# Layer 0's feed-forward and half of its return gathers are placed between the steps of layer 1's attention

## The chip, the core and the metric

The kernel runs on one core of a Trainium2 chip. The core has five engines that run side by side, each through its own instructions in order: TensorE (PE in the profile; its weight loads are PEld), VectorE (DVE), ScalarE (ACT), GpSimd (POOL) and SyncE (SP, which here only issues DMAs). Matrix products land in PSUM, which has 8 banks of 128 x 512 floats; everything else is in SBUF. The metric is the device time of one execution in microseconds (us), and the median of nine runs is taken.

## What is computed

A stack of four "gated" layers runs over x, 16 batches of 128 tokens with 128 features, with a context of the same shape. Each layer adds tanh(gate) times a cross-attention block and then tanh(gate) times a feed-forward block, both of a layer norm of x. The part that matters here is:

```
x = x + tanh(g_xattn[0]) * L0_xattn(layernorm(x), ctx)   # top 2 of 8 experts for each token
x = x + tanh(g_ffn[0])   * L0_ffn(layernorm(x))          # relu, hidden values rounded to fp8, output to fp16
x = x + tanh(g_xattn[1]) * L1_xattn(layernorm(x), ctx)   # 16 heads of 8, softmax in blocks of 64 keys
x = x + tanh(g_ffn[1])   * L1_ffn(layernorm(x))          # 8 components, the largest logit chooses
```

Layer 0's first block routes each token, by its context row, to two of eight experts. Its feed-forward has 512 hidden values. Layer 1's attention has 16 heads over 128 keys, with a maximum and a sum for each block of 64 keys. Layer 2 needs a table of position vectors, which are gathered row by row long before it and turned (transposed) on the way.

## The kernel before, in words

The 16 batches are taken in 4 chunks of 4 (NJ = 4, BJ = 4). The program is written in Tile: the order of the instructions on each engine is chosen by a scheduler from the order in the text and from its own estimates, except where a wrapper (class `InOrder`, L28) tells it to keep the order of the text. Before, only layer 1's feed-forward and one later layer are wrapped.

**Layer 0's experts** (`l0_xattn`, L293). The tokens are sorted by expert into 39 blocks of 128 rows. A one-hot tile `of` (L388) is built to find each block's tokens; 32 matmuls read it. Then for each block the rows are gathered by GpSimd (L454), the expert's first weights are fetched by SyncE into a ring of 7 (`w1`, L438, 258 KB each), and the result rows are written to a buffer in HBM (L499).

**The way back** (`l0_returned`, L506). For a batch b, GpSimd gathers from that buffer the rows of each token's first and second expert (two gathers, L512), and VectorE adds each, weighted, to x[b] (L519). A gather is told to start only behind the addition two before it (`k.behind`, L516), and there are 4 buffers.

**Layer 0's feed-forward** (`l0_ffn`, L544), chunk by chunk. `hidden(j)` norms the chunk (`layernorm`: statistics, a square root on ScalarE, xn on VectorE, four transposes, a copy), multiplies it by the first weights (4 matmuls of 128 x 512) and rounds to fp8 on ScalarE. `output(j)` has 16 fp8 matmuls, an addition of the bias (`l0f_y`) and an addition to x. Chunk 0's return gathers stand ahead of the loop; the gathers of the following chunk stand between the matmuls of each chunk, and 6 of the 17 turns of positions (`turn_positions`) too. PSUM is split here into 4 + 2 + 2 banks.

**Layer 1's attention** (`l1_xattn`, L593), one pass over 16 batches in eight stages, each some steps behind the one before, with all 8 banks in one rotation. In the prediction the stages go by the names of their tiles:

- `queries` (L670): every fourth step, `project` norms the next chunk and computes its queries and keys (matmuls by Wq and Wk), `project_values` the values; in every step, GpSimd spreads queries and keys over the heads (`l_qz`, `l_kz`, L663).
- `maxima` (L681): scores by 4 matmuls, then four reductions on VectorE into `l_top` (L690). Each step releases one gather of position rows (`pe<-in_L_xattn_rpe`, L961; `k.gather`).
- `turned`: `l_top` is transposed, copied by ScalarE, and GpSimd makes `l_mz` of it (L703).
- `weights` (L708): scores minus maxima by 8 matmuls, exponentials on ScalarE (`l_a`, L722).
- `values`, `normed` (divides by the sums, `l_y`, L748, and releases another gather of position rows), `output`, `projected` (matmul by Wo, addition to x).

Layer 1's feed-forward (`l1_ffn`) follows. There GpSimd subtracts and adds in pairs, VectorE takes a running maximum of which each releases a gather of position rows as long as any of the 65 is left, and the rest of the turns lie between.

Of the kernel before, what the change touches and what calls it, by code (L numbers as in the profile page):

```python
# [18 lines left out]
P = 128  # L19
NB = 16  # L20
# [7 lines left out]
class InOrder:  # L28


    def __init__(self, tc, engine):
        self.tc, self.engine, self.last = tc, engine, None
# [18 lines left out]
class Engines:  # L51


    def __init__(self, tc, nc):
        self.nc = nc
        self.tensor, self.vector, self.scalar, self.gpsimd = (
            InOrder(tc, e) for e in (nc.tensor, nc.vector, nc.scalar, nc.gpsimd)
        )

    def __getattr__(self, name):  # L60
        return getattr(self.nc, name)
# [2 lines left out]
class Kernel:  # L64
# [27 lines left out]
        return self.psum.tile([P, 512], F32, tag=tag, name=f"ps_{tag}", bufs=self.bufs[tag])  # L92

    def w2k(self, name):
        return self.work.tile([P, 512], F32, tag="w2k", name=name, bufs=13)

    def sq(self, name, dtype=F32):
        return self.small.tile([P, P], dtype, tag="sq", name=name, bufs=14)
# [182 lines left out]
def pipeline(n, *stages):  # L281


    kept = {}
    for t in range(n + max(lag for _, lag in stages)):
        for s, (fn, lag) in enumerate(stages):
            u = t - lag
            if 0 <= u < n:
                kept[u, s] = fn(u, kept.pop((u, s - 1))) if s else fn(u)
# [3 lines left out]
def l0_xattn(k):  # L293
# [91 lines left out]

    blockb = k.sm([P, 2 * NB], "l0_blockb", BF16, bufs=1)
    nc.vector.tensor_copy(blockb, block)
    of = k.work.tile([P, 2 * NB, 2, NBLK], BF16, tag="l0_of", name="l0_of", bufs=1)  # L388
    nc.vector.tensor_tensor(
        of[:, :, 1], bc(along[:, 0:NBLK].unsqueeze(1), [P, 2 * NB, NBLK]), bc(blockb.unsqueeze(2), [P, 2 * NB, NBLK]),  # L390
        ALU.is_equal,
# [114 lines left out]
def l0_returned(k, b):  # L506


    nc = k.nc
    for i in range(2):  # L510
        y = k.small.tile([P, P], F32, tag="l0_xs", name="l0_back", bufs=4)
        dma = nc.gpsimd.indirect_dma_start(  # L512
            out=y, out_offset=None, in_=k.l0_out_d,
            in_offset=bass.IndirectOffsetOnAxis(ap=k.l0_rows[:, 2 * b + i : 2 * b + i + 1].bitcast(U32), axis=0),
        )
        if len(k.l0_added) > 1:  # L516
            k.behind(dma, k.l0_added[-2])
        k.l0_added.append(
            nc.vector.scalar_tensor_tensor(  # L519
                k.x[:, b, :], y, k.l0_w[:, b, i : i + 1], k.x[:, b, :], ALU.mult, ALU.add  # L520
            )
        )
# [21 lines left out]
def l0_ffn(k):  # L544

    nc = k.nc
    w1 = k.load("L0_ffn_w1T", [P, 512], tag="ffn_w1")
    b1 = k.load("L0_ffn_b1T", [P, NF])  # L550
    w2 = k.load("L0_ffn_w2T", [P, NF, P], "(c p) d -> p c d", tag="ffn_w2", p=P)
    b2 = k.load_rows("L0_ffn_b2", P, tag="ffn_b2")
    wq, bq = k.wts.tile([P, NF, P], FP8, name="l0_wq"), k.wts.tile([P, P], F16, name="l0_bq")
    nc.vector.tensor_copy(wq, w2, saturate=False)
    nc.vector.tensor_copy(bq, b2)
    k.l0_added = []
    l2_gates_of_ctx(k)
    for b in range(BJ):
        l0_returned(k, b)

    def hidden(j):
        k.layernorm(j)
        hq = k.work.tile([P, NF, N], FP8, tag="w4k", name="l0f_q", bufs=3)
        for f in range(NF):
            ph = k.ps("mm")
            k.mm(ph, w1[:, f * P : (f + 1) * P], k.chunk(k.xnT, j))
            nc.scalar.activation(hq[:, f, :], ph, AF.Relu, bias=b1[:, f : f + 1], saturate=False)
            if j + 1 < NJ:
                l0_returned(k, BJ * (j + 1) + f)
            if j and f % 2:  # L570
                turn_positions(k, 2 * (j - 1) + f // 2)
        return hq

    def output(j, hq):
        py = k.ps("acc")
        for i in range(BJ):
            for f in range(NF):
                k.mm(
                    py[:, i * P : (i + 1) * P], hq[:, f, i * P : (i + 1) * P], wq[:, f, :],
                    start=f == 0, stop=f == NF - 1,  # L580
                )
        y = k.work.tile([P, N], F16, tag="w2k", name="l0f_y", bufs=13)
        nc.vector.tensor_tensor(
            y.rearrange("p (b d) -> p b d", b=BJ), py.rearrange("p (b d) -> p b d", b=BJ),
            bc(bq.unsqueeze(1), [P, BJ, P]), ALU.add,
        )
        k.add_chunk(j, y, 4)

    pipeline(NJ, (hidden, 0), (output, 1))

def l1_xattn(k):  # L593

# [3 lines left out]


    nc = k.nc
    k.banks(bank=8)
    H, DH, G = 16, 8, 4
    scale = DH**-0.5
    wq, wk, wv, wo = (k.load(f"L1_xattn_W{n}T", [P, P], tag=f"W{n}") for n in "qkvo")
    by_h = lambda t: t.rearrange("p (h s) -> p h s", h=4)
    neg = k.const.tile([P, 4], F32, name="l1_neg")

    nc.gpsimd.memset(neg, -1.0)  # L610
    for g in range(G):
        rows = neg[32 * g : 32 * g + 32, :]
        nc.gpsimd.affine_select(
            out=rows, in_=rows, pattern=[[-2, 4]], compare_op=ALU.is_ge, fill=0.0, base=0, channel_multiplier=1
        )
        nc.gpsimd.affine_select(
            out=rows, in_=rows, pattern=[[2, 4]], compare_op=ALU.is_ge, fill=0.0, base=1, channel_multiplier=-1
        )

# [13 lines left out]
    two = k.wts.tile([P, 2, BJ, H, 32], F32, tag="w16b", name="l1_v")  # L633
    vs = [two[:, n] for n in range(2)]
    for v in vs:
        nc.gpsimd.memset(v, 0.0)
        nc.gpsimd.memset(v[0:64, :, :, DH : DH + 1], 1.0)
        nc.gpsimd.memset(v[64:P, :, :, 2 * DH + 1 : 2 * DH + 2], 1.0)
    qkT = {}

    def project(j):
        k.layernorm(j)
        qkT[j] = (k.w2k("l1_qT"), k.w2k("l1_kT"))
        for out, w, src in zip(qkT[j], (wq, wk), (k.xnT, k.ctxT)):
            pq = k.ps("mm")
            k.mm(pq, w, k.chunk(src, j))
            nc.scalar.copy(out, pq)
# [20 lines left out]
        return out  # L668

    def queries(b):  # L670
        if b == 0:
            project(0)
            project_values(0)
        if b % BJ == 2 and b // BJ + 1 < NJ:
            project(b // BJ + 1)
        if b % BJ == 3 and b // BJ + 1 < NJ:

            project_values(b // BJ + 1)
        return masked(b)

    def maxima(b, qk):  # L681
        qz, kz = qk
        j, i = divmod(b, BJ)
        top = tops[b % 3]
        ss = [k.ps("mm") for _ in range(G)]
        for g in range(G):
            rows = slice(32 * g, 32 * g + 32)
            k.mm(ss[g], qkT[j][0][rows, i * P : (i + 1) * P], kz[rows, :])
        for g in range(G):
            done = nc.vector.tensor_reduce(  # L690
                top[:, 32 * g : 32 * g + 8], ss[g].rearrange("p (n s) -> p n s", n=8), AX.X, ALU.max
            )
        k.gather(done)
        return qz, top

    def turned(b, qt):
# [82 lines left out]
    for t in range(NB + 6):  # L779
        for fn, lag in stages:  # L780
            b = t - lag
            if 0 <= b < NB:
                args = (state.pop((after[fn], b)),) if fn in after else ()
                state[fn, b] = fn(b, *args)
        if t == NB + 1:

            xn = k.work.tile([P, BJ, P], F32, tag="w4k", name="l1f_xn", bufs=3)
            k.layernorm(0, keep=xn, pow=k.half)

def l1_ffn(k):
# [105 lines left out]
    for s in range(C * NJ + 24):  # L898
# [19 lines left out]
        for m, i in ms:  # L918
# [9 lines left out]
            elif i == C + 3:  # L928
                for fn, half in (
# [1 line left out]
                    (added, 1),  # L931
                ):
                    fn(m, half)
        if s % 2 and s // 2 <= P // 8 - 6:
            turn_positions(k, s // 2 + 6)
        for n in pieces.get(s, []):
            if n not in under_way:
                under_way[n] = k.norm(n[1], pow=k.half)
# [774 lines left out]
        k.add_chunk(j, y, 7)  # L1713


LAYERS = [l0_xattn, l0_ffn, l1_xattn, l1_ffn, l2_xattn, l2_ffn, l3_xattn]


@with_exitstack
# [83 lines left out]
```

## Time and profile before

| | |
|---|---|
| median of 9 runs | 903.63 us (899.38 to 908.04) |
| the profiled execution | 905.5 us, of which the profile's span is 903.7 us |
| mean granted TensorE clock | 0.911 of full speed |
| experts, to the last result row | to 131.6 us |
| return gathers and layer 0's feed-forward | 136 to 207 us |
| layer 1's attention | 205 to 346 us |
| layer 1's feed-forward | 346 to 450 us |
| busy, TensorE / VectorE / ScalarE / GpSimd | 80% / 57% / 44% / 47% of the span |

Times in the views count from the span's start. A line of the timeline gives start and duration, the engine, the line of the kernel, the operation, the tile that is written and those that are read, and how many instructions were merged; in brackets stands how long the engine had been idle and what released it. A matmul of floats counts twice, since it runs in two passes. The buffer numbers of tiles are left out, and layer numbers in names are cut to "l_". Lines of the stages' table give start and end, length, busy time and count of each engine, the granted clock as a share of full speed, the share of the DMA engines and GB/s.

### The profile page before, as it was taken

What the parts mean: (1) busy time and instruction counts of PE and PEld (TensorE: products, weight loads), DVE (VectorE), ACT (ScalarE), POOL (GpSimd) and SP (SyncE); (2) the same over time, 40 slices, a digit from 0 to 9 for tenths busy, and PEclk for the clock granted to TensorE, in tenths of its full rate; (3) what the DMA queues carried; (4) which work ended last, traced back from release to release, by engine and by line L of the source; (5) the groups of instructions that cost most, each with busy time, mean ns of one, the idle gap of its engine ahead of it and who ended that gap; (6) DMA issues with size and microseconds to landing.
All of it is one profiled execution on the core that took longest, in us unless ns stands there. A gap on an engine that the chain in (4) does not pass through costs nothing.

```text
span 903.7 us, 13278 instructions
## 1 busy us (share of the span) xinstructions
PE 724.8 (80%) x4349; PEld 486.3 (54%) x4349; DVE 517.4 (57%) x1462; ACT 401.5 (44%) x1006; POOL 421.6 (47%) x443
## 2 busy tenths in 40 slices
PE   3289981565897999799487899966899975999997
PEld 3179980332454555344287633334678864656555
DVE  6735543555645546879967135575711464777863
ACT  0035531342533545776226705632545443676552
POOL 6666645623744864777266405441200232555430
PEclk9989995877989999999859899995899996999999
DMA  8758751100000000000303113330000000000001
GB/s 254 206 133 224 205 136 38 39 18 15 18 13 19 25 22 21 0 1 0 93 1 105 51 31 109 95 127 1 1 1 0 1 2 0 1 1 1 1 1 47
DMA packets 43654, 46.49 MB, mean 51 GB/s; under 512 B 8369, under 2 KB 32561, under 8 KB 43457
## 3 DMA queue, kind: packets, MB, share of 16 engines
q1 hardware_dynamic: 37088, 35.63, 13.4%
q0 software_dynamic: 4384, 8.95, 4.3%
q10 hardware_dynamic: 2112, 1.05, 0.4%
q8 instruction: 35, 0.57, 0.3%
q14 instruction: 35, 0.28, 0.1%
HBM read 40.90 MB, written 4.72 MB: 50 GB/s over the span
## 4 chain that ended last, share of the span: by engine, by line
PE 50%; DVE 21%; POOL 8%; issue 7%; ACT 6%; DMA 3%; SPq 0%; ACTq 0%; DVEq 0%; POOLq 0%
PE ps_bank L112 16%; PE ps_bank L38 14%; PE ps_mm L112 12%; PE ps_acc L112 5%; POOL l_back L512 2%; DMA l_back<-l_out_d,l_rows 2%; DVE l_m L38 2%; DVE xn L38 2%; DVE l1f_r L38 1%; ACT l_cm L1154 1%; POOL l_ss L1211 1%; PE ps_bank L116 1%; DVE xn L215 1%; PE ps_tr L116 1%; DVE xnT L38 1%
## 5 line engine op out<-in xcount | busy, mean ns | idle before, releaser
L961 POOL DMA_INDIRECT pe<-in_L_xattn_rpe,itokT x65 | 64.3, 990 | 65.9 <-DVE l_top L690 24.7
L38 PE MATMUL ps_bank<-xnT,l1f_w 128*128 128x512 f32 x128 | 59.8, 594 | 0.4 <-ACT pe L38 0.4
L112 PE MATMUL ps_mm<-pe,ident 128*128 128x512 f32 x64 | 59.4, 1050 | 0.0
L690 DVE TENSOR_REDUCE l_top<-ps_bank 128x8 f32<-128x512 f32 x64 | 39.8, 684 | 33.5 <-PE ps_bank L112 33.5
L722 ACT ACTIVATE l_a<-ps_bank 128x512 f32<-128x512 f32 x64 | 33.2, 604 | 45.4 <-PE ps_bank L112 45.3
L484 DVE TENSOR_SCALAR l_h<-ps_mm,l_w 128x128 f32<-128x128 f32 x117 | 33.7, 344 | 33.1 <-ACT l_h L486 31.8
L1154 ACT ACTIVATE l_cm<-l_cm,l_g 128x128 f32<-128x128 f32 x128 | 39.4, 393 | 24.3 <-POOL l_cm L1147 24.3
L454 POOL DMA_INDIRECT l_xs<-l_rows_d,l_tok x39 | 37.1, 951 | 21.5 <-PE ps_acc L112 14.2
L112 PE MATMUL ps_acc<-l_w,l_h 128*128 128x128 f32 x312 | 45.6, 280 | 1.6 <-ACT l_w L471 1.3
L1147 POOL TENSOR_SCALAR_AFFINE_SELECT l_cm<-l_cm 128x512 f32<-128x512 f32 x32 | 23.6, 758 | 46.0 <-PE ps_mm L112 32.9
L112 PE MATMUL ps_mm<-l_xT,l_w 128*128 128x128 f32 x312 | 44.3, 280 | 0.4 <-ACT l_xT L469 0.4
L512 POOL DMA_INDIRECT l_back<-l_out_d,l_rows x32 | 31.1, 971 | 26.6 <-DVE x L519 19.3
L112 PE MATMUL ps_mm<-l_qz,pe 128*128 128x128 f32 x256 | 37.5, 313 | 6.7 <-ACT pe L1101 6.7
L112 PEld LDWEIGHTS ps_acc<-l_w,l_h 128*128 128x128 f32 x312 | 40.0, 193 | 2.5 <-ACT l_w L471 1.5
L1326 ACT ACTIVATE l2f_h<-ps_bank,sb_L_ffn_b1T 128x264 f32<-128x264 f32 x64 | 28.3, 482 | 28.4 <-PE ps_bank L112 28.3
L112 PEld LDWEIGHTS ps_mm<-l_xT,l_w 128*128 128x128 f32 x312 | 40.0, 196 | 0.6 <-ACT l_xT L469 0.6
L112 PEld LDWEIGHTS ps_mm<-l_qz,pe 128*128 128x128 f32 x256 | 36.0, 226 | 7.5 <-ACT pe L1101 7.5
L1335 DVE TENSOR_SCALAR l2f_y<-ps_bank,sb_L_ffn_b2T 128x264 f32<-128x264 f32 x16 | 7.9, 493 | 49.7 <-PE ps_bank L112 49.7
L38 PE MATMUL ps_bank<-xnT,sb_L_xattn_gru_whT 128*128 128x512 f32 x72 | 35.8, 607 | 0.0
L38 POOL TENSOR_TENSOR ln_rs<-ln_rs,neg_half 128x4 f32<-128x4 f32 x14 | 14.7, 1051 | 44.6 <-DVE ln_rs L38 39.4
L38 PEld LDWEIGHTS ps_bank<-xnT,l1f_w 128*128 128x128 f32 x128 | 22.9, 191 | 23.3 <-issue 16.6
L1211 POOL TENSOR_TENSOR l_ss<-l_ss,neg_half 128x16 f32<-128x16 f32 x8 | 23.3, 2913 | 26.0 <-DVE l_ss L1210 26.0
(422 smaller groups left out, 1966.4 us busy)
## 6 DMA issues: line engine op xcount, KB each, us to landing
l_w<-in_L_xattn_w1b SPq DMA_DIRECT2D x39, 258.0 KB
l_cm<-l_gm_d SPq DMA_DIRECT2D x64, 128.0 KB
l_out_d<-l_y SPq DMA_DIRECT2D x39, 64.0 KB
sb_L_xattn_W<-in_L_xattn_W SPq DMA_DIRECT2D x1, 2048.0 KB
sb_L_ffn_w<-in_L_ffn_w SPq DMA_DIRECT2D x1, 2048.0 KB
pe<-in_L_xattn_rpe,itokT POOLq DMA_INDIRECT x65, 2.6
x<-in_x ACTq DMA_DIRECT2D x4, 256.0 KB
ctxT<-in_ctxT SPq DMA_DIRECT2D x1, 1024.0 KB
```

The source lines that it names most:

```text
L38: done = op(*args, **kw)
L112: self.nc.tensor.matmul(out, lhsT, rhs, start=start, stop=stop)
L454: nc.gpsimd.indirect_dma_start(out=xs, out_offset=None, in_=rows_d, in_offset=bass.IndirectOffsetOnAxis(ap=tok[:, n : n + 1].bitcast(U32), ...
L484: nc.vector.tensor_scalar(h[:, cols], ph[:, cols], bias, 0.0, ALU.add, ALU.max)
L512: dma = nc.gpsimd.indirect_dma_start(out=y, out_offset=None, in_=k.l0_out_d, in_offset=bass.IndirectOffsetOnAxis(ap=k.l0_rows[:, 2 * b + i ...
L690: done = nc.vector.tensor_reduce(top[:, 32 * g : 32 * g + 8], ss[g].rearrange("p (n s) -> p n s", n=8), AX.X, ALU.max)
L722: nc.scalar.activation(a, ss[g], AF.Exp, scale=scale)
L961: dma = nc.gpsimd.indirect_dma_start(out=k.pe[:, g if g < G - 1 else P - 1, :], out_offset=None, in_=k.a["L2_xattn_rpe"], in_offset=bass.I ...
L1147: nc.gpsimd.affine_select(out=by_n(cm), in_=by_n(cm), pattern=[[0, 4], [1, P]], compare_op=ALU.is_ge, fill=1e30, base=0, channel_multiplie ...
L1154: nc.scalar.activation(part, part, AF.Exp, scale=-1.0, bias=g[:, n : n + 1])
L1211: nc.gpsimd.tensor_tensor(ss, ss, half, ALU.pow)
L1326: nc.scalar.activation(h, ph, AF.Gelu, bias=b1[:, e * NF + f : e * NF + f + 1])
```

## The change

Layer 0's feed-forward is no longer a loop of its own. `l0_ffn` gathers the first two chunks' returns and makes 7 turns of positions; then it hands its two stages, `hidden` and `output`, to `l1_xattn`. That calls both for chunk 0 ahead of the first projection. The gathers of batch 8 + t stand at the end of step t, for t from 0 to 7; chunk j + 1's `hidden` stands at the end of step 4j, and its `output` at the end of step 4j + 1.

GpSimd's order is told from there on (the wrapper takes one engine's name alone). Constants and memsets of layer 1 go around the wrapper, and so do the gathers of position rows. Only gathers 3 to 16 are spread behind additions. The norms of all chunks but the first use a power on GpSimd instead of ScalarE's square root. In the first half of attention, `maxima` releases no position rows. PSUM becomes one rotation of 8 banks ahead of layer 0's feed-forward. There are 15 work buffers of 128 x 512 floats, not 13, and the one-hot tile `of` shares the buffer of the experts' weights ring. Layer 1's feed-forward begins with turn 7, not 6.

```diff
-    of = k.work.tile([P, 2 * NB, 2, NBLK], BF16, tag="l0_of", name="l0_of", bufs=1)
+    of = k.wts.tile([P, 2 * NB, 2, NBLK], BF16, tag="w16a", name="l0_of")
...
-        if len(k.l0_added) > 1:
+        if len(k.l0_added) in range(2, 4 * BJ):
             k.behind(dma, k.l0_added[-2])
...
     k.l0_added = []
+    k.banks(bank=8)
+
+    k.nc = Engines(k.tc, k.nc, ("gpsimd",))
     l2_gates_of_ctx(k)
-    for b in range(BJ):
+    for b in range(2 * BJ):
         l0_returned(k, b)
 
+    for n in range(7):
+        turn_positions(k, n)
+
     def hidden(j):
-        k.layernorm(j)
+        k.layernorm(j, pow=k.half if j else None)
...
-            if j + 1 < NJ:
-                l0_returned(k, BJ * (j + 1) + f)
-            if j and f % 2:
-                turn_positions(k, 2 * (j - 1) + f // 2)
         return hq
...
-    pipeline(NJ, (hidden, 0), (output, 1))
+    return hidden, output
...
-def l1_xattn(k):
+def l1_xattn(k, ffn):
...
-    k.banks(bank=8)
...
     def project(j):
-        k.layernorm(j)
+        k.layernorm(j, pow=k.half if j else None)
...
     def queries(b):
+        j, i = divmod(b, BJ)
         if b == 0:
+            ffn[1](0, ffn[0](0))
             project(0)
             project_values(0)
...
-        k.gather(done)
+        if b >= NB // 2:
+            k.gather(done)
...
                 state[fn, b] = fn(b, *args)
+        j, i = divmod(t, BJ)
+        if t < 2 * BJ:
+            l0_returned(k, 2 * BJ + t)
+        if j + 1 < NJ:
+            if i == 0:
+                hq[0] = ffn[0](j + 1)
+            if i == 1:
+                ffn[1](j + 1, hq.pop(0))
...
+    k.nc = k.nc.nc
...
-        if s % 2 and s // 2 <= P // 8 - 6:
-            turn_positions(k, s // 2 + 6)
+        if s % 2 and s // 2 <= P // 8 - 7:
+            turn_positions(k, s // 2 + 7)
...
+def l0_ffn_l1_xattn(k):
+    l1_xattn(k, l0_ffn(k))
```

The listing of the changed kernel's instructions, which can be read before it runs, shows the order on each engine that follows from this. TensorE has, from the end of the experts: the gates of the context, 28 transposes for the turns, chunk 0's feed-forward and projection, the transposes and first layer of feed-forward chunk 1, the scores of batch 0, the second layer of chunk 1, the projection of chunk 1, the scores of batch 1, and so on. GpSimd has 16 return gathers, `l_qz` and `l_kz` of batch 0, then in each step two return gathers after `l_mz`, the power of a norm where one is due, `l_qz`, `l_kz`, one or two gathers of position rows, and the next `l_mz`. VectorE has each pair of additions among the reductions of the following batch, or ahead of the xn of a feed-forward chunk.

More of the change, by code (lines that the diff above doesn't have):

```diff
@@ L51, with __init__ @@
 class Engines:
-    def __init__(self, tc, nc):
+    def __init__(self, tc, nc, names=("tensor", "vector", "scalar", "gpsimd")):
         self.nc = nc
-        self.tensor, self.vector, self.scalar, self.gpsimd = (
-            InOrder(tc, e) for e in (nc.tensor, nc.vector, nc.scalar, nc.gpsimd)
-        )
+        for name in names:
+            setattr(self, name, InOrder(tc, getattr(nc, name)))
     def __getattr__(self, name):
@@ L94, in w2k @@
     def w2k(self, name):
-        return self.work.tile([P, 512], F32, tag="w2k", name=name, bufs=13)
+        return self.work.tile([P, 512], F32, tag="w2k", name=name, bufs=15)
     def sq(self, name, dtype=F32):
@@ L581, in output @@
                 )
-        y = k.work.tile([P, N], F16, tag="w2k", name="l0f_y", bufs=13)
+        y = k.work.tile([P, N], F16, tag="w2k", name="l0f_y", bufs=15)
         nc.vector.tensor_tensor(
@@ L608, in l1_xattn @@
     neg = k.const.tile([P, 4], F32, name="l1_neg")
-    nc.gpsimd.memset(neg, -1.0)
+    k.nc.nc.gpsimd.memset(neg, -1.0)
     for g in range(G):
         rows = neg[32 * g : 32 * g + 32, :]
-        nc.gpsimd.affine_select(
+        k.nc.nc.gpsimd.affine_select(
             out=rows, in_=rows, pattern=[[-2, 4]], compare_op=ALU.is_ge, fill=0.0, base=0, channel_multiplier=1
         )
-        nc.gpsimd.affine_select(
+        k.nc.nc.gpsimd.affine_select(
             out=rows, in_=rows, pattern=[[2, 4]], compare_op=ALU.is_ge, fill=0.0, base=1, channel_multiplier=-1
@@ L635, in l1_xattn @@
     for v in vs:
[L636 to L639, printed above, removed]
+        k.nc.nc.gpsimd.memset(v, 0.0)
+        k.nc.nc.gpsimd.memset(v[0:64, :, :, DH : DH + 1], 1.0)
+        k.nc.nc.gpsimd.memset(v[64:P, :, :, 2 * DH + 1 : 2 * DH + 2], 1.0)
+    qkT, hq = {}, {}
     def project(j):
-        k.layernorm(j)
+        k.layernorm(j, pow=k.half if j else None)
         qkT[j] = (k.w2k("l1_qT"), k.w2k("l1_kT"))
@@ L670, in queries @@
     def queries(b):
+        j, i = divmod(b, BJ)
         if b == 0:
+            ffn[1](0, ffn[0](0))
             project(0)
             project_values(0)
[L674 to L678, printed above, removed]
+        if i == 2 and j + 1 < NJ:
+            project(j + 1)
+        if i == 3 and j + 1 < NJ:
+            project_values(j + 1)
         return masked(b)
@@ L1713, in output @@
         k.add_chunk(j, y, 7)
-LAYERS = [l0_xattn, l0_ffn, l1_xattn, l1_ffn, l2_xattn, l2_ffn, l3_xattn]
+def l0_ffn_l1_xattn(k):
+    l1_xattn(k, l0_ffn(k))
+LAYERS = [l0_xattn, l0_ffn_l1_xattn, l1_ffn, l2_xattn, l2_ffn, l3_xattn]
 @with_exitstack
```

## The prediction

> **What bounds the kernel now.** I read the page's slices first (22.6 us each), then the busy times by stage, then GpSimd's and TensorE's instructions in order of time from 130 to 346 us, which is all that the change touches before layer 1's feed-forward.
>
> ```profile
> PE   3289981565897999799487899966899975999997
> POOL 6666645623744864777266405441200232555430
> PEclk9989995877989999999859899995899996999999
> ```
>
> TensorE is the bound nearly everywhere, but slices 7 to 12 are thin. GpSimd's rows say why:
>
> ```profile
> 136.24 0.95 POOL L512 DMA_INDIRECT l_back<-l_out_d,l_rows  x1 [3.42 <-issue]
> ...
> 161.47 0.95 POOL L512 DMA_INDIRECT l_back<-l_out_d,l_rows  x1 [0.97 <-DVE x L519]
> ...
> 189.51 0.95 POOL L512 DMA_INDIRECT l_back<-l_out_d,l_rows  x1 [1.05 <-DVE x L519]
> 209.46 1.04 POOL L663 TENSOR_TENSOR l_qz<-l_qT,mask8x 128x512 f32<-128x512 f32 x1 [19.00 <-ACT ln_rs L259]
> ```
>
> The 32 return gathers take 136.2 to 192 us, one by one, and layer 0's feed-forward runs in their shadow, chunk by chunk. Attention's first masked query comes at 209.5. I measure attention by its beats: m(b) is the start of the GpSimd product l_mz of batch b. Before, m(0) to m(15) stand at 217.1, 230.2, 235.7, 240.8, 247.4, 262.8, 269.8, 277.2, 283.3, 298.3, 305.3, 311.2, 317.3, 323.4, 329.5 and 335.6. A plain beat takes 6.1 us; the beats in which the next chunk is projected take 13.1, 15.4 and 15.0. There TensorE runs dry:
>
> ```profile
> 244.89 0.27 PE L116 MATMUL ps_bank<-ident,l_top 128*128 128x128 f32 x1
> 246.45 0.75 PE L116 MATMUL ps_bank<-ident,xn 128*128 128x128 f32 x3 [1.29 <-DVE xn L215]
> 248.63 0.48 PE L116 MATMUL ps_bank<-ident,xn 128*128 128x128 f32 x1 [1.43 <-DVE xn L215]
> 249.78 2.07 PE L112 MATMUL ps_bank<-xnT,sb_L_xattn_WqT 128*128 128x512 f32 x2 [0.68 <-ACT xnT L107]
> ```
>
> It takes its instructions in order, so the next scores wait behind the projection's transposes, and those wait for xn. After the hole the clock is down too (columns: stage, its length, busy and count of PE, PEld, DVE, ACT, POOL, clock, DMA):
>
> ```profile
> 250.00:260.00 10.00, 10.00 (x68) 4.81 (x69) 2.64 (x5) 2.48 (x5) 1.74 (x2) 0.74 0.02 4
> 315.00:345.00 30.00, 27.93 (x329) 18.31 (x327) 14.90 (x42) 14.34 (x37) 18.42 (x19) 1.00 0.09 23
> ```
>
> **What goes.** Attention now needs 16 gathers, not 32. Addition 16 ran at 164.05. Feed-forward chunk 0 is unchanged until then (its fp8 matmuls end at 163.0). After it come l0f_y and its addition (0.69 + 0.74), 8 statistics (2.6, as at 183.45), square root and xn (2.0), and from the transposes to the end of l_kz 6.9 us as now (205.26 to 212.1): l_kz ends at 177, not 212. That is 35 us, but the first beat does not get them. In the changed kernel's order, TensorE has the transposes and the first layer of feed-forward chunk 1 ahead of batch 0's scores, and GpSimd issues gathers 17 and 18 after l_kz and before the power of chunk 1's norm. A gather's data can be used 2.5 us after its start:
>
> ```profile
> DMA to landing us min/median/max: 2.4/2.5/2.6
> ```
>
> and two in a row start 1.26 apart (136.24, 137.50). So additions 17 and 18 run at 179.6 and 180.9, and VectorE has both ahead of xn. Then xn collides with GpSimd's next two products:
>
> ```profile
> 215.75 4.47 DVE L215 TENSOR_SCALAR xn<-x,ln_mv,ln_rs 128x128 f32<-128x128 f32 x4
> ...
> L215 DVE TENSOR_SCALAR xn<-x,ln_mv,ln_rs x36: 317/341/3682, 153.4 to 455.1; 128x128 f32<-128x128 f32 x36
> ```
>
> Four take 1.1 us alone and 4.5 beside products: one sat 3.68 us until GpSimd's run ended. So xn ends at 183, its copy at 184.2; the first layer takes 4.15 (the row at 182.43, clock 0.74); scores at 188.5, maxima 2.5, transpose, copy: m(0) at 192.4, against 217.1. **Gain 24.7.**
>
> The Trainium skill (SBUF — State Buffer, "Who interferes with whom") makes the shared port pair an exclusive lock held for a whole instruction. By that rule one xn would wait for one product, some 1.0 us; the 3.68 us row shows the wait lasting over a run of them. By the rule alone the five later norms would cost some 1 us less each.
>
> **What comes into the beats**, by the changed order (t from the beat's own start):
>
> - m(0) to m(1), chunk 1's second layer and projection. The fp8 matmuls end at 0.6, l0f_y and addition at 2.0, statistics stop for gather 19 (GpSimd: product 1.04, pause 0.16, so it starts at 1.2 and lands at 3.75), the power runs 4.5 to 5.5, the next l_qz and l_kz until 7.6, xn 8.2, transposes and copy 9.2, Wq and Wk 3.3 (221.62 to 224.93), then 5.25 from the scores to the beat as now: 17.9, was 13.1. **+4.8.**
> - m(1) to m(3). VectorE has additions 21 and 22 after the first of the four maxima of batch 2, 23 and 24 after the second of batch 3. They land at 3.75 and 5.05, where the maxima now end near 2.1. With the maxima left behind them, transpose, copy and the product start: 8.2 and 7.75, were 5.6 and 5.0. **+5.3.**
> - m(3) to m(4), chunk 2's first layer. Additions 25 and 26 until 5.4, the power until 4.5, products until 7.6, xn 7.9, copy 8.8, first layer 13.0; only then the scores of batch 4, and 8.7 from there to the beat (9.3 from 253.49 to 262.83; here the output projection's matmuls are not under way yet): 21.7, was 6.7. **+15.0.**
> - m(4) to m(5), second layer and projection: power 4.4 to 5.5, products 7.6, copy 9.2, Wq and Wk 12.6, then 9: 21.6, was 15.4. **+6.2.**
> - m(5) to m(7): two return gathers take the place of one rpe gather; 3 products, 2 returns, 1 rpe are 6.8 us of GpSimd, under the 7.0 and 7.4 now. **+0.2.**
> - m(7) to m(8), chunk 3's first layer without gathers: power 2.1, products 4.2, xn 4.8, copy 5.7, first layer 9.9, then 8.7: 18.6, was 6.1. **+12.5.**
> - m(8) to m(9), as m(4): 21.5, was 15.0. **+6.5.**
> - m(9) to m(15) holds the same work as now: 0.
>
> **The rest.** The one-hot tile l_of now lies in the buffer of the expert weights, so the first of them is fetched when its matmuls end (43.96), not at 34.61. The expert stage starts at 50.05, on a gather that lands at 49.2, and seven fetches (1.8 MB, 4 to 9 us at 200 to 400 GB/s) now run beside those gathers. Bounds 0 and 9.4; I take 1.0, near 0, since only 258 KB are needed by 50. Eight rpe gathers move into layer 1's feed-forward, four of them past GpSimd's subtractions; GpSimd idles 5.1 us at 366.4. Bounds 0 and 8 x 1.26; I take 1.5. The seven turns of positions run while TensorE is idle (132 to 153): 0, and if that cover fails 7 x 1.0. One bank rotation and 15 work buffers: 0, no row waits for one.
>
> **The sum:** -24.7 + 1.0 + 4.8 + 5.3 + 15.0 + 6.2 + 0.2 + 12.5 + 6.5 + 1.5 = +28.3. The profiled execution took 905.5 (span 903.7), so 933.8; the median of the runs shown, 903.6, lies 1.9 lower: 931.9, and I forecast **930**. With xn never blocked (2 us less at each of five norms) and the first layer at the full clock (0.5 less at three) the sum is +16.8, 920.5; with every xn blocked 3.7 and the first layer at the cold 5.6 (the row at 155.7) about +38, 942. Fetches and rpe gathers at their far ends would add up to 17.
>
> **Rivals.**
> 1. Holes no deeper than a projection's now (about 11 us over four plain beats: 35.5 between m(5) and m(9) against 24.4). It needs the norm's power and additions to be early, so that VectorE's waits cost nothing: 3 x 11 - 24.7 + 2.5 = +10.8, **914**. For it: the first beats hold few stages. Against it: the told order puts the power after the gathers.
> 2. Faster. The feed-forward fills the holes and costs only its matmuls, 3 x 6 us (1.0 transposes, 4.15, 0.9). Then -24.7 + 18 + 1 = about -6, **898**. The place is TensorE's row ahead of batch 4's scores; it decides for this if xn of chunk 2 is ready when batch 3's maxima are transposed, that is, if additions 25 and 26 land before m(3) and not after it. Against it: they are issued after m(3) in the listing. The skill (Perfetto Trace Analysis, "Optimization Strategy") says that interleaving stages with different busiest engines may gain, and it speaks for this rival; no row shows such a gain in this kernel.
> 3. The change does less than it says: attention starts early but the gain and the new waits meet near zero, **903**. That would take half of each hole.
>
> **How the numbers follow.** The forecast has 0.55, rival 1 0.20, rival 2 0.20, rival 3 0.05. Slower by over 0.3% (2.7 us, about what a measurement of this kernel can tell from no change) is the forecast and rival 1: 0.75; within 0.3% 0.05; faster 0.20. The range 898 to 945 takes in rival 1, half of rival 2 and the walk's own bounds (920 to 942, a little more for fetches); some 0.17 is left out.
>
> **What would show it.** In the changed profile, l_kz of batch 0 ends near 178 and m(0) near 193; from there each step can be read off: beats of about 18, 22, 22, 19 and 22 us where a chunk's feed-forward or projection lies, TensorE waiting on xn for 7 to 9 us ahead of the first layer, VectorE's additions waiting for l_back between maxima, m(15) near 362. Wrong, if TensorE's holes are shorter than 4 us; if xn stays at 0.3 us; if the expert stage starts past 52.

## The result, and the profile after

The changed kernel takes **957.1 us** in the median of 14 runs (954.2 to 958.4), beside 903.6 in 46 runs of the kernel before: 1.0588 times as long (95% interval 1.0568 to 1.0608). The forecast was 930, the range ended at 945. The sign was right, the loss nearly twice as large as predicted: +53.5 where +28.3 was summed.

The page's slices of the changed kernel (23.9 us each):

```profile
PE   2279983555586699869957879995879985999997
POOL 6656645225343375784626550435120042365530
PEclk9979995677777799989987889997599997999999
```

The thin part of TensorE now lasts from slice 7 to slice 14, the clock is lower in it (0.5 to 0.7), and there is a second thin place at slice 18, in layer 1's feed-forward, of which the forecast knew nothing.

I cut every execution at the same four landmarks: first return gather, m(0), m(15), last addition of layer 1's feed-forward. Lengths in us, from each run's profiled execution ("the rest" runs from that last addition to the end; what lies ahead of the first return gather is not in the table):

| kernel | ratio to before (95%) | returns to m(0) | m(0) to m(15) | layer 1's feed-forward | the rest |
|---|---|---|---|---|---|
| before | 1 | 80.9 | 118.5 | 114.7 | 453.4 |
| changed | 1.0588 (1.0568 to 1.0608) | 58.7 | 176.0 | 128.4 | 454.6 |
| e0 changed again | 1.0582 (1.0529 to 1.0636) | 58.7 | 175.6 | 128.3 | 454.5 |
| e1 side edits alone | 0.9959 (0.9927 to 0.9992) | 80.1 | 116.0 | 114.9 | 451.1 |
| e2 all returns ahead | 1.0409 (1.0359 to 1.0458) | 64.6 | 158.6 | 128.5 | 452.6 |
| e3 position gathers as before | 1.0361 (1.0319 to 1.0404) | 58.9 | 175.0 | 115.0 | 458.5 |
| e4 xn by ScalarE | 1.0491 (1.0442 to 1.0540) | 61.2 | 183.6 | 118.4 | 451.0 |
| e5 norm ahead of gathers | 1.0395 (1.0348 to 1.0442) | 54.3 | 169.8 | 125.5 | 453.5 |
| e6 = e3 + early norms | 1.0119 (1.0069 to 1.0169) | 50.5 | 155.7 | 117.5 | 456.4 |
| e7 = e1 + early norms | 0.9934 (0.9908 to 0.9960) | 82.7 | 109.4 | 115.0 | 454.4 |
| e8 GpSimd waits for xn | 1.0432 (1.0373 to 1.0491) | 58.3 | 179.0 | 116.2 | 456.4 |
| e9 = e7 + e8's wait | 0.9971 (0.9945 to 0.9996) | 83.3 | 105.7 | 115.8 | 454.0 |
| e10 = e9, returns less spread | 0.9825 (0.9786 to 0.9864) | 73.6 | 105.0 | 115.6 | 453.0 |
| e11 = e6 + e5 + e8 | 1.0137 (1.0084 to 1.0189) | 48.9 | 158.1 | 115.8 | 453.2 |
| e12 four gathers withheld | 1.0485 (1.0437 to 1.0532) | 58.5 | 173.3 | 121.1 | 454.5 |
| e13 six gathers withheld | 1.0473 (1.0424 to 1.0522) | 57.5 | 177.2 | 118.8 | 455.6 |
| e14 before, eight withheld | 1.0075 (1.0047 to 1.0103) | 78.6 | 115.3 | 124.3 | 454.1 |

e1 to e8 ran on two chips on which the kernel before takes 917 to 919 us; the first return gather of these eight came at 147 to 152, not at 136 to 140, so the experts' stage ahead of the table is some 10 us longer there. Absolute times in the expectations are meant for the first chip; I compare by stage and by ratio. Between runs even a stage that an edit leaves alone differs by some 3 us (e8 edits only layer 1's feed-forward, and its attention takes 179.0, the changed kernel's 176.0), so differences of that size in attention say little.

The sum for the change itself: experts +2.2, returns to m(0) -22.2, attention +57.5, layer 1's feed-forward +13.7, the rest +1.2: +52.4 from these rounded terms, and 52.3 is the difference of the two spans (956.05 and 903.72).

**The start** went as predicted: GpSimd's timeline in the changed kernel,

```profile
177.73 1.04 POOL L38 TENSOR_TENSOR l_kz<-l_kT,mask8x 128x512 f32<-128x512 f32 x1 [0.59 <-ACT l_kT L649]
178.91 0.98 POOL L38 DMA_INDIRECT l_back<-l_out_d,l_rows  x1
180.20 0.96 POOL L38 DMA_INDIRECT l_back<-l_out_d,l_rows  x1 [0.31 <-issue]
181.17 1.05 POOL L38 TENSOR_TENSOR ln_rs<-ln_rs,neg_half 128x4 f32<-128x4 f32 x1
182.21 1.03 POOL L38 TENSOR_TENSOR l_qz<-l_qT,mask8x 128x512 f32<-128x512 f32 x1
183.21 1.03 POOL L38 TENSOR_TENSOR l_kz<-l_kT,mask8x 128x512 f32<-128x512 f32 x1
```

and VectorE's beside it:

```profile
182.77 1.62 DVE L518 SCALAR_TENSOR_TENSOR x<-l_back,l_w,x 128x128 f32<-128x128 f32 x1 [1.04 <-DMA l_back<-l_out_d,l_rows]
184.31 1.10 DVE L214 TENSOR_SCALAR xn<-x,ln_mv,ln_rs 128x128 f32<-128x128 f32 x4
```

l_kz of batch 0 ends at 178.8 (178 was predicted). What stands still beside the products is the return's addition: 1.62 us instead of 0.35, until l_kz ends at 184.2. xn comes after it, unhindered (1.10). The prediction had the wrong victim, though the delay was about right.

**The holes** are there too: TensorE waits 6.4, 7.7 and 3.9 us for xn ahead of the three first layers of chunks 1 to 3, and 6.4, 7.3 and 6.4 us ahead of their projections. Two of the six, in TensorE's timeline of the changed kernel:

```profile
241.44 1.15 PE L115 MATMUL ps_bank<-ident,xn 128*128 128x128 f32 x4 [7.70 <-DVE xn L214]
243.27 6.74 PE L111 MATMUL ps_bank<-xnT,sb_L_ffn_w1T 128*128 128x512 f32 x8 [0.68 <-ACT xnT L106]
...
263.31 1.15 PE L115 MATMUL ps_bank<-ident,xn 128*128 128x128 f32 x4 [7.34 <-DVE xn L214]
```

Ahead of the first layers 7 to 9 us had been predicted; one of the three comes up to that. VectorE's timeline shows why the xn of the first of these two holes is late:

```profile
237.96 0.35 DVE L518 SCALAR_TENSOR_TENSOR x<-l_back,l_w,x 128x128 f32<-128x128 f32 x1 [3.75 <-DMA l_back<-l_out_d,l_rows]
239.16 1.88 DVE L518 SCALAR_TENSOR_TENSOR x<-l_back,l_w,x 128x128 f32<-128x128 f32 x1 [0.85 <-DMA l_back<-l_out_d,l_rows]
240.96 1.11 DVE L214 TENSOR_SCALAR xn<-x,ln_mv,ln_rs 128x128 f32<-128x128 f32 x4
```

It stands behind two return additions, which wait for their gathers' data, and the second of which takes 1.88 us beside a product of GpSimd, not 0.35; the xn itself is not held up. The first layer after the hole takes 6.74 us, not the 4.15 that I took. The stages' table of the changed kernel around its second and third first layer,

```profile
243.00:250.00 7.00, 6.73 (x12) 2.58 (x12) 0.00 (x0) 2.28 (x4) 0.78 (x1) 0.54 0.00 0
301.00:308.00 7.00, 6.65 (x9) 2.53 (x10) 0.00 (x0) 2.36 (x4) 0.79 (x1) 0.54 0.00 0
```

and of the kernel before around the one from which the 4.15 came,

```profile
182.00:187.00 5.00, 4.74 (x14) 2.30 (x13) 4.25 (x24) 3.14 (x6) 2.33 (x3) 0.85 0.10 26
```

have the reason in the third number from the end, the granted clock: 0.54 now, 0.85 there. Over the rows themselves it is 0.54 and 0.87, and time by clock is the same: 6.74 x 0.54 and 4.15 x 0.87 both give 3.6.

**The second thin place.** VectorE's timeline in layer 1's feed-forward of the changed kernel:

```profile
416.60 0.75 DVE L38 SCALAR_TENSOR_TENSOR l1f_top<-ps_bank,sb_L_ffn_sel_bT,l1f_top 128x512 f32<-128x512 f32 x1 [1.10 <-ACT pe L38]
417.26 11.15 DVE L38 TENSOR_SCALAR xn<-x,ln_mv,ln_rs 128x128 f32<-128x128 f32 x4
428.33 0.68 DVE L38 COPY_PREDICATED ps_bank<-l1f_odd,ps_bank 128x512 f32<-128x512 uint32 x1
```

Four xn take 11.15 us (10.38 of them the first alone) where the kernel before needs 4.28 at the same place:

```profile
378.20 4.28 DVE L38 TENSOR_SCALAR xn<-x,ln_mv,ln_rs 128x128 f32<-128x128 f32 x4
```

GpSimd's timeline beside the long wait, in the changed kernel:

```profile
409.63 0.94 POOL L975 DMA_INDIRECT pe<-in_L_xattn_rpe,itokT  x1 [0.30 <-DVE ln_st L38]
410.58 1.05 POOL L38 TENSOR_TENSOR ln_rs<-ln_rs,neg_half 128x4 f32<-128x4 f32 x1
...
425.08 2.47 POOL L38 TENSOR_TENSOR pe<-pe,l1f_top 128x512 f32<-128x512 f32 x2
437.80 1.27 POOL L38 TENSOR_TENSOR l1f_e<-l1f_e 128x512 f32<-128x512 f32 x1 [10.24 <-ACT l1f_e L38]
```

Its instructions follow each other from 409.6 to 427.55, and the first xn ends 0.1 us after that run. TensorE's timeline:

```profile
429.07 1.11 PE L38 MATMUL ps_bank<-ident,xn 128*128 128x128 f32 x4 [8.63 <-DVE ps_bank L38]
```

TensorE waits 8.63 us ahead of these transposes, for the copy that VectorE makes after xn; at the same place of the kernel before it waits 1.77. In the whole stage TensorE is idle for 29.0 us instead of 20.8, and busy for 99.4 instead of 93.9 at a granted clock of 0.91 instead of 0.98: these two differences, 8.2 and 5.5, are the 13.7 us.

### The profile page after: what moved, and what is told of

The parts are those of the page before. It is cut to its first block, busy times and chain, and to the rows that moved or that the text cites. A ratio compares the mean times of both kernels' runs of the same rounds, so it can differ in the third digit from the quotient of the medians.

```text
span 956.1 us, 13253 instructions
## 1 busy us (share of the span) xinstructions
PE 740.3 (77%) x4349; PEld 492.0 (51%) x4349; DVE 525.4 (55%) x1456; ACT 400.9 (42%) x1000; POOL 427.0 (45%) x449
## 4 chain that ended last, share of the span: by engine, by line
PE 47%; DVE 20%; issue 8%; POOL 8%; DMA 5%; ACT 5%; SPq 1%; ACTq 0%; DVEq 0%; POOLq 0%
PE ps_bank L111 15%; PE ps_bank L38 15%; PE ps_mm L111 10%; PE ps_acc L111 5%; DMA l_back<-l_out_d,l_rows 3%; PE ps_bank L115 2%; DVE xn L38 2%; POOL l_back L38 2%; DVE l_m L38 2%; POOL l_mz L38 1%; DVE l1f_r L38 1%; POOL l_ss L1225 1%; ACT l_cm L1168 1%; DMA l_cm<-l_gm_d 1%; DVE xnT L38 1%
## 5 line engine op out<-in xcount | busy, mean ns | idle before, releaser
L38 PE MATMUL ps_bank<-xnT,l1f_w 128*128 128x512 f32 x128 | 65.0, 639 | 0.0
L111 PE MATMUL ps_mm<-pe,ident 128*128 128x512 f32 x64 | 58.9, 1050 | 0.0
L115 PE MATMUL ps_bank<-ident,xn 128*128 128x128 f32 x36 | 10.9, 451 | 61.1 <-DVE xn L214 61.1
L1161 POOL TENSOR_SCALAR_AFFINE_SELECT l_cm<-l_cm 128x512 f32<-128x512 f32 x32 | 21.9, 700 | 58.7 <-DMA l_cm<-l_gm_d 58.2
L518 DVE SCALAR_TENSOR_TENSOR x<-l_back,l_w,x 128x128 f32<-128x128 f32 x32 | 18.7, 586 | 45.6 <-DMA l_back<-l_out_d,l_rows 45.4
L38 POOL TENSOR_TENSOR ln_rs<-ln_rs,neg_half 128x4 f32<-128x4 f32 x21 | 22.1, 1051 | 39.9 <-DVE ln_rs L38 34.9
L115 PEld LDWEIGHTS ps_bank<-ident,xn 128*128 128x128 f32 x36 | 6.5, 182 | 64.7 <-issue 46.5
L1192 DVE TENSOR_TENSOR l_cm<-ps_mm,l_cm 128x512 f32<-128x512 f32 x32 | 21.9, 688 | 30.3 <-PE ps_mm L111 18.4
```

The lines of the kernel that those rows point to most:

```text
L38: done = op(*args, **kw)
L111: self.nc.tensor.matmul(out, lhsT, rhs, start=start, stop=stop)
L115: self.nc.tensor.transpose(out, in_, self.ident[:n, :n])
L1161: nc.gpsimd.affine_select(out=by_n(cm), in_=by_n(cm), pattern=[[0, 4], [1, P]], compare_op=ALU.is_ge, fill=1e30, base=0, channel_multiplie ...
L1192: nc.vector.tensor_mul(cms[w], ps[w], cms[w])
```

## The experiments

**e1: are the side edits dear?** The kernel before with `of` moved, one bank rotation from `l0_ffn` on, 15 buffers, and the seven turns ahead of the feed-forward (these lines are in the diff of the change).

> The kernel before with the change's side edits alone: the one-hot tile in the weights' ring, one rotation of 8 banks from layer 0's feed-forward on, 15 work buffers, seven turns of positions ahead of the feed-forward. Theory (the loss lies between attention's beats and in GpSimd's backlog behind them, the side edits cost only the experts' 2.2 us): 904 to 907 us, with the xn of layer 1's feed-forward waiting 4.3 us at most, as before. Rival (the side edits carry the 14.9 us lost after m(15)): 913 or more, with an xn of some 10 us in layer 1's feed-forward.

The ratio is 0.996: the side edits cost nothing, and the whole is some 4 us faster, where no change to 3 us more had been expected. The two long xn of layer 1's feed-forward take 4.27 and 4.29. The rival falls.

**e2: returns or feed-forward?**

```diff
-    for b in range(2 * BJ):
+    for b in range(NB):
         l0_returned(k, b)
...
-        if t < 2 * BJ:
-            l0_returned(k, 2 * BJ + t)
```

> The changed kernel with all 32 return gathers ahead of attention; only layer 0's feed-forward stays between the beats. Theory (each feed-forward stage between beats is a hole by itself; the returns cost their additions and the power's place behind them): m(0) near 211, the two beats m(5) to m(7) back at 7.0 and 7.4 from 9.8 and 10.1, the beats with feed-forward or projection still 15 to 19.5, so m(15) 363 to 369 and 945 to 955 us. Rival (the returns alone make the loss, the feed-forward between the beats is free without them): beats of chunks 2 and 3 as before, m(0) to m(15) near 125, about 920 us.

m(0) 213.5 on this chip, 64.6 after the first gather. m(5) to m(7) is 13.2 us (7.1 and 6.1), not 19.8; the beats with a feed-forward or a projection stay at 18.1 to 19.5. So the returns between the beats give 5.9 us at the start and cost 17.4 later, a net loss of 11.5. Without them, with the feed-forward stages still between the beats, attention is 40 us longer than before (158.6 to 118.5). The theory holds; the time, 1.041, came out a little under its range.

**e3: the withheld position gathers.**

```diff
-        if b >= NB // 2:
-            k.gather(done)
+        k.gather(done)
```

> The changed kernel with position gathers released in every batch's maxima again, as before. Theory (eight gathers moved into layer 1's feed-forward put GpSimd behind, so that its instructions run back to back and VectorE's xn at 417 waits 10.4 us for the end of that run): that xn ends within 4.5 us and layer 1's feed-forward is 8 to 11 us shorter; the first eight beats get up to 1.3 us longer each, so 946 to 955 us. Rival (layer 1's feed-forward is late for another reason, the turns or the bank rotation): the stage stays 10 us longer, and the whole comes to 957 to 965 us.

Layer 1's feed-forward is back at 115.0 (13.4 less, where 8 to 11 had been expected), and attention does not pay for it: 175.0, not 176.0. The long xn in VectorE's timeline of e3:

```profile
425.02 4.29 DVE L38 TENSOR_SCALAR xn<-x,ln_mv,ln_rs 128x128 f32<-128x128 f32 x4
```

The withholding was pure loss. In the changed kernel GpSimd stood idle for 3.3 to 3.6 us ahead of three of the position gathers that were left between m(4) and m(7).

**e4: xn taken from VectorE**, from layer 0's feed-forward to layer 1's feed-forward (the switch that limits it to these is left out here):

```diff
+            sh = self.sm([P, BJ], "ln_sh")
+            nc.vector.scalar_tensor_tensor(sh, mv[:, :, 0], -1.0, rs, ALU.mult, ALU.mult)
...
+                nc.scalar.activation(
+                    xn[:, i, :], self.x[:, BJ * j + i, :], AF.Identity, bias=sh[:, i : i + 1], scale=rs[:, i : i + 1]
+                )
```

> The changed kernel with xn of layer 0's feed-forward, layer 1's attention and layer 1's feed-forward made by ScalarE (a scale and a shift), not by VectorE. Theory (VectorE's xn is shut out as long as GpSimd's instructions follow each other without a pause): the 10.4 us wait in layer 1's feed-forward goes and xn takes 1.2 to 2 us there, that stage is 7 to 9 us shorter, the attention 0 to 3 us: 945 to 951 us. Rival (xn waits for something that VectorE has no part in, its statistics or the power): xn takes as long on ScalarE, and the time stays within 2 us of 957.

Four xn on ScalarE take 1.65 us in each of the 15 norms, GpSimd's products beside them or not, and layer 1's feed-forward is 10.0 shorter. But attention is 7.6 longer, which the theory did not expect. The returns' additions are still held up there, by up to 2.84 us, and ScalarE is busy for 66.6 us of the stage, not 58.2; which of the two costs the time is not shown.

**e5: the norm ahead of the gathers.**

```diff
-        if t < 2 * BJ:
-            l0_returned(k, 2 * BJ + t)
         if j + 1 < NJ:
...
                 ffn[1](j + 1, hq.pop(0))
+        if t < 2 * BJ:
+            l0_returned(k, 2 * BJ + t)
```

> The changed kernel with the feed-forward's stage called ahead of the return gathers in each step, so that the power of the norm goes to GpSimd ahead of two gathers, and xn to VectorE ahead of two additions. The changed kernel stands at 1.059 times the kernel before. Theory (the told order makes two of the three first-layer holes deeper, by two gathers of 1.26 us and by the additions that are shut out beside products): 3 us less in each of the two, ratio 1.050 to 1.054. Rival (the norm waits for something else, its statistics or the second layer): no change, ratio 1.057 to 1.061.

The stretch from the returns to m(0) is 4.4 us shorter and attention 6.2 (m(3) to m(4) takes 17.0, not 22.7). The hole of chunk 2's first layer, TensorE's timeline of e5:

```profile
243.28 1.30 PE L115 MATMUL ps_bank<-ident,xn 128*128 128x128 f32 x4 [2.94 <-DVE xn L214]
245.25 5.70 PE L111 MATMUL ps_bank<-xnT,sb_L_ffn_w1T 128*128 128x512 f32 x8 [0.68 <-ACT xnT L106]
```

TensorE waits 2.94 us here, not 7.70, and 2.27 instead of 6.38 ahead of chunk 1's first layer. The order told to GpSimd cost 10.6 us in these two stretches, more than the 3 us in each of two holes that I had expected, and the ratio is below my range.

**e6 and e7: norms one step or two ahead of their matmuls.** In e6, on top of e3:

```diff
-        if i == 2 and j + 1 < NJ:
-            project(j + 1)
-        if i == 3 and j + 1 < NJ:
-
-            project_values(j + 1)
...
-            if i == 0:
-                hq[0] = ffn[0](j + 1)
-            if i == 1:
-                ffn[1](j + 1, hq.pop(0))
+            if i in (0, 2):
+                if i == 2:
+                    ffn[1](j + 1, hq.pop(0))
+                steps[0] = k.norm(j + 1, pow=k.half)
+                next(steps[0])
+                next(steps[0])
+            if i == 1:
+                hq[0] = ffn[0](j + 1, steps[0])
+            if i == 3:
+                project(j + 1, steps[0])
+                project_values(j + 1)
```

(`hidden` and `project` then only run the norm's last step, the transposes. The norms begin no earlier than in the changed kernel: it is the transposes and matmuls that come one step after them.) In e7, on top of e1:

```diff
-        if b % BJ == 2 and b // BJ + 1 < NJ:
-            project(b // BJ + 1)
+        if b % BJ == 1 and b // BJ + 1 < NJ:
+            steps[0] = k.norm(b // BJ + 1, pow=k.half)
+            next(steps[0])
+            next(steps[0])
         if b % BJ == 3 and b // BJ + 1 < NJ:
+            project(b // BJ + 1, steps[0])
```

> The kernel of e3 (position gathers as before, 1.036) with each norm (statistics, power, xn) started one step ahead of its transposes and matmuls, for layer 0's feed-forward and for the projections alike. Theory (TensorE takes its instructions in order and stands 35 to 40 us ahead of transposes whose xn is late; the matmuls themselves cost little): 20 to 35 us less, ratio 0.998 to 1.015. Rival (the holes come from GpSimd's products and VectorE's additions that the scores wait for anyway, or from the lower clock, so they open again elsewhere): less than 8 us, ratio above 1.027.

> The kernel of e1 (the kernel before with the side edits, 0.996), with the norms of layer 1's projections started two steps ahead of their transposes, by a power on GpSimd. Theory (the three beats with a projection, 14.0, 9.4 and 13.5 us in e1 against 6.1 for a plain one, hold 3 to 4 us of TensorE waiting for xn, except the second): 5 to 9 us less, ratio 0.986 to 0.991. Rival (the wait for xn is replaced by a wait of the products or the scores): ratio 0.994 to 0.998.

e6, beside e3, takes 19.3 us less in attention, 8.4 less ahead of it and 2.5 more in layer 1's feed-forward. TensorE's waits for xn of over 1.5 us inside attention's beats and just ahead of them add up to 9.8 us, against 41.8 in e3 and 38.0 in the changed kernel (six waits, 3.9 to 7.7 each). So in-order TensorE behind a late xn was the main cost in attention. e7, beside e1, takes 6.6 less in attention and loses 2.6 ahead of it; the ratio falls between the two expectations.

**e8: a wait added.** In layer 1's feed-forward, GpSimd's next subtraction waits for the norm's last xn:

```diff
-        engine.tensor_tensor(d, d, tops[j], ALU.subtract)
+        done = engine.tensor_tensor(d, d, tops[j], ALU.subtract)
+        if engine is nc.gpsimd and k.last_xn is not None:
+            k.behind(done, k.last_xn)
+            k.last_xn = None
```

> The changed kernel (1.059) with one wait added to each norm inside layer 1's feed-forward: GpSimd's next subtraction waits for the norm's last xn, so that GpSimd's row of instructions has a gap there. Theory (VectorE's xn is shut out until GpSimd's instructions leave a gap, for 10.4 us at 417): xn takes under 2.6 us, GpSimd loses 1 to 2 us per norm, layer 1's feed-forward is 5 to 9 us shorter, ratio 1.049 to 1.053. Rival (what VectorE gains GpSimd loses, or xn waits for something else): ratio 1.057 to 1.062.

The stage is 12.2 us shorter, where 5 to 9 had been expected, and the ratio is below my range. VectorE's timeline and GpSimd's in e8:

```profile
434.10 1.38 DVE L38 TENSOR_SCALAR xn<-x,ln_mv,ln_rs 128x128 f32<-128x128 f32 x4
```

```profile
433.37 1.26 POOL L38 TENSOR_TENSOR l1f_e<-l1f_e 128x512 f32<-128x512 f32 x1
435.56 2.51 POOL L38 TENSOR_TENSOR pe<-pe,l1f_top 128x512 f32<-128x512 f32 x2 [0.94 <-DVE xn L38]
```

The four xn take 1.38 us instead of 11.15, and GpSimd pays 0.94 of waiting. Since a wait on GpSimd's side is enough to let xn through, GpSimd's row is what had kept it out, and no missing input.

**e0, e9, e10, e11.** e0 is the changed kernel again. e9 is e7 with e8's wait, e10 is e9 with `if len(k.l0_added) in range(2, 4 * BJ)` in place of `> 1`, e11 is e6 with e5's order and e8's wait.

> The changed kernel once more, unedited, as the base for the other runs: 1.053 to 1.059 times the kernel before. The stages of the runs so far, put beside those of the changed kernel's first profile, give 1.053 here; the first comparison gave 1.0588. Either way the differences of e2, e3, e5 and e8 to it should come to 10 to 18 us.

> The kernel of e7 (the kernel before with the side edits and early norms, 0.993) with the wait of e8 in layer 1's feed-forward. Theory (two norms of that stage are shut out for 4.3 us each, of which 3 are TensorE's loss only where its row runs dry, 1.8 us at most): xn at 1.1 to 2.6 us, that stage 1 to 4 us shorter, ratio 0.989 to 0.992. Rival (GpSimd's lost time costs as much): 0.993 to 0.996.

> The kernel of e9 with only the first 16 return gathers told to start behind additions, as in the changed kernel. Theory (in e2 all 32 gathers took 45.8 us from first to last, in the kernel before 53.3, and layer 0's feed-forward follows them): attention starts 5 to 7 us earlier, ratio 0.982 to 0.986. Rival (the feed-forward's own chain of four chunks, not the gathers, sets when attention starts): no change against e9.

> The kernel of e6 (1.012: the changed kernel with position gathers as before and early norms), with the norms ahead of the return gathers in each step and the wait of e8. Theory (power and xn ahead of gathers and additions saved 10 us in e5, of which early norms have taken most; GpSimd itself is the bound now, with 8 to 9 us of products, gathers and powers in each of the first eight beats): 3 to 7 us less than e6, ratio 1.004 to 1.009, so the feed-forward between the beats stays behind the kernel that has it ahead of attention. Rival (nothing but order was wrong with the change): under 0.99, ahead of e9.

e9 missed both of its ranges: the wait brings nothing where xn is held up 4.3 us only (the stage takes 115.8, and 115.0 without it). e10 is as expected and **beats both kernels: 888.5 us, 0.9825**. Its returns end 45.8 us after the first, not 53.3, so attention starts 7.3 us earlier than before (9.7 earlier than in e9, where 5 to 7 had been expected), and takes 13.5 less than before. It has the side edits of e1 too. e11 stays behind the kernel before, as expected, but its 1.0137 is above the range and no better than e6, and the reason given was wrong: its GpSimd is busy for 56 of the 97 us of the first eight beats and no bound, by the stages' table of e11:

```profile
188.70:285.40 96.70, 70.60 (x566) 39.23 (x566) 56.02 (x126) 36.01 (x72) 56.28 (x58) 0.82 0.08 20
```

No engine is full in it (TensorE, first in the row, is at 73%, at a clock of 0.82). What makes a beat of e11 12 us long is not settled.

**e12, e13, e14: what makes xn wait for eight instructions?** The bound in `maxima` at 4 and at 6 in the changed kernel; and, in e14, at 8 in the kernel before with nothing else changed.

> The changed kernel with position gathers withheld in the first 4 batches' maxima, not 8. If the wait grows with GpSimd's lateness: xn of layer 1's feed-forward waits 6 to 8 us and the stage (15th beat to its last addition, 128.4 us with eight withheld, 115.0 with none) takes 120 to 123. If it is a switch: 10.4 us and 126 to 128, or 4.3 us and 115 to 117.

> The changed kernel with position gathers withheld in the first 6 batches' maxima. If the wait grows with GpSimd's lateness: xn waits 8 to 10 us and the stage takes 123 to 126. If it is a switch: 10.4 us and 127 to 128, or 4.3 us and 115 to 118.

> The kernel before with position gathers withheld in the first 8 batches' maxima, and nothing else changed. Theory (the withholding alone brings the loss, wherever layer 0's feed-forward lies): the stage takes 126 to 129 us, not 114.7, one xn waits some 10 us, attention gains nothing or up to 2 us, ratio 1.010 to 1.016. Rival (it needs the changed kernel's turns and order as well): the stage 115 to 118, ratio 0.998 to 1.004.

At the place of the long wait the four xn take 4.28 with four withheld and 4.28 with six, 11.15 with eight: for that wait, nearer to a switch than to growth. The stage fits neither: 121.1 with four lies in the range that I gave for growth, 118.8 with six in none, and none, four, six and eight withheld (115.0, 121.1, 118.8, 128.4) make no steady growth. With four withheld an earlier xn, at 399.4, waits 4.25 us by itself. So a single wait can last one, three or eight GpSimd instructions. In e14, VectorE's timeline has

```profile
374.70 11.15 DVE L38 TENSOR_SCALAR xn<-x,ln_mv,ln_rs 128x128 f32<-128x128 f32 x4
```

with 10.38 for the first xn, and the stage is 9.6 us longer than in the kernel before: the withholding alone brings the long wait, without the moved feed-forward. e14 gets 5.5 us back ahead of that stage; its stage (124.3) and its ratio are a little below the ranges that I gave. What decides how many instructions a wait lasts is left open.

## Why the prediction was wrong

Point by point (us; predicted, measured):

| step | predicted | measured |
|---|---|---|
| experts, by `of` | +1.0 | +2.2 |
| m(0) | 193.4 | 197.1 |
| m(0) to m(1) | 17.9 | 19.3 |
| m(1) to m(3) | 16.0 | 17.8 |
| m(3) to m(4) | 21.7 | 22.7 |
| m(4) to m(5) | 21.6 | 19.6 |
| m(5) to m(7) | 14.6 | 19.8 |
| m(7) to m(8) | 18.6 | 19.5 |
| m(8) to m(9) | 21.5 | 18.6 |
| m(9) to m(15) | 37.3 | 38.8 |
| layer 1's feed-forward | +1.5 | +13.7 |
| the rest | 0 | +1.2 |

For attention the forecast's mechanism was right in the main: TensorE in order, xn late, holes (of 3.9 to 7.7 us), and the told order that puts power and xn behind gathers (e5, e6). What makes xn late was in part wrong: I charged 2 us in each of five norms for xn shut out beside products, but in four of the six norms in and just ahead of the beats the four xn take 1.1 us, and in two of these an addition ahead of xn is held up instead (1.62 and 1.88 us). Of the eight terms for the beats, seven are within 3 us, some of them by luck: in the two beats with a first layer the 2.6 us that it took too long are partly made up by what follows it, 6.8 and 7.7 us where I had taken 8.7.

- **The step that failed** is "Eight rpe gathers move into layer 1's feed-forward ... I take 1.5", with bounds 0 and 8 x 1.26. I counted the gathers' own time, and the bounds with it. The stage measured 13.7. With the gathers in it GpSimd comes 1.5 us later to its power (410.58, 37.5 after m(15), against 36.0 before), and one xn waits 10.4 us. I had read the lock from a row in attention (4.47 us at 215.75); a row of its kind, 4.28 us at 378.2, stood in that very stage of the kernel before, and I did not carry the lock there. That the gathers bring the long wait is shown by e3 and e14, and that the wait makes the loss by e8: 12 us of the 24 missed. Why the wait jumps to eight instructions stays open.
- **m(5) to m(7), "+0.2"**: I asked only whether GpSimd had room for the returns. It has. But VectorE has the two additions between its reductions, first waiting for the data and then for the products:

```profile
280.20 1.86 DVE L518 SCALAR_TENSOR_TENSOR x<-l_back,l_w,x 128x128 f32<-128x128 f32 x1 [2.11 <-DMA l_back<-l_out_d,l_rows]
```

```profile
282.72 0.49 PE L111 MATMUL ps_bank<-sb_L_xattn_WoT,l_yT 128*128 128x128 f32 x2 [1.56 <-DVE l_top L694]
...
292.96 0.49 PE L111 MATMUL ps_bank<-sb_L_xattn_WoT,l_yT 128*128 128x128 f32 x2 [2.81 <-DVE l_top L694]
```

  2.11 us for the gather and 1.86 for an addition of 0.35, then TensorE for the maxima. (VectorE's line above, then TensorE's, in the changed kernel.) I had this very wait in m(1) to m(3) and did not repeat it here: +5.2. e2, without returns in the beats, has 13.2 there.
- **m(0) and the first layers**: 4.15 us was taken for a first layer, the rows say 6.06, 6.74 and 6.72, at a clock of 0.61, 0.54 and 0.54: 2 to 2.6 us each. The clock of 0.74 that I put beside the 4.15 belongs to another stretch (250 to 260 us); over that row it is 0.87, so I took a nearly full clock for a first layer behind a hole. The bound of 5.6, from a row at 0.65, was too low as well.
- **m(4) to m(5) and m(8) to m(9)** came out 2.0 and 2.9 shorter: their four xn took 1.1 us, not blocked, where I had charged 2 more.
- **The side edits at nothing** held (e1). The rest of the kernel moved by 1.2, within what two executions differ by.
- **The experts** came out 1.2 dearer than taken: the first transpose waits 7.14 us for its gathered rows (l_xs), not 4.59, and the first expert matmul starts at 52.84, not 50.05.
- **The upper bound:** 3.7 in place of 2 at five norms and 5.6 in place of 4.15 at three first layers give +41 by these terms, not about +38.

Of the signs that were to show the forecast wrong, two came about, the expert stage past 52 and xn at 0.3 us apiece in most norms; of the six holes one, 3.91, is under 4 us.

Rival 2 (898) was to be decided by whether additions 25 and 26 come before m(3), so that xn is ready. They run 3.8 and 5.0 us after it. e6 and e11 put a step between xn and its transposes, by which e6 gains 28 us up to m(15) over e3, yet they stay 1 to 1.4% behind the kernel before, so that condition alone was not enough. Rival 1 (914, holes no deeper than a projection's) describes e6 (1.012 times the kernel before) fairly well, but not the changed kernel. Rival 3 falls.

On the lock, the Trainium skill (SBUF — State Buffer, "Who interferes with whom") says that the pair of ports is held for a whole instruction, and that VectorE's instructions with two SBUF inputs contend too with GpSimd instructions that read SBUF. The additions agree with the second (1.62 to 1.86 us beside products, 0.35 alone). The xn of the kernel before at 378.2 agree with the first: four of them took 4.28 us while four GpSimd instructions of 1.25 passed. The xn at 417.3 waited for eight, so a wait can last over many instructions of an unbroken run and not only over the one under way; there the measurement decides.

## What to carry to other kernels

Work that is moved into another stage brings its norms' latency with it: if an in-order engine meets its first matmul before the vector chain ahead of it is done, the stage is a hole and not a filling, and a step between that chain and the matmuls took back 28 us up to the end of attention here (e6), and 6.6 us in attention of the kernel before (e7). When gathers are pushed from one stage to another, look at the place where they land, and at which of VectorE's instructions stand beside GpSimd's unbroken rows there; a wait added to GpSimd at the right place can cost 1 us and save 12 (e8), or save nothing where the waits were short (e9). Try the cheap part by itself: early norms and less spread returns, with the side edits and without moving the feed-forward at all, gave 0.9825 (e10).

## What the runs showed of the hardware that I had not expected

- One 128x128 xn on VectorE took 10.37 to 10.38 us, over eight GpSimd instructions in a row, in five runs (the changed kernel, e0, e2, e5 and e14), while with slightly different timing (the kernel before, e3, e12) four xn each waited for one instruction, 4.28 us in all. A wait added to GpSimd brought the 11.15 us of four xn down to 1.38 (e8).
- Five of the returns' additions of two SBUF tiles on VectorE stretched from 0.35 to 1.6 to 1.9 us beside GpSimd's products in the changed kernel, none in the kernel before; xn moved to ScalarE (e4) took 1.65 us for four in all 15 norms.
- The eight matmul passes of a first layer took 6.06 to 6.74 us at a granted clock of 0.54 to 0.61 in attention's beats, and from 3.99 at 0.90 to 5.62 at 0.65 in the kernel before: time by clock is 3.6 to 3.7 in each.
- A wait of VectorE for GpSimd lasted one, three (4.25 us, e12) or eight instructions for the same operation on the same shapes.
